# First key block ahead of the queries, and the last shared-expert batch added to the output in one transfer

## The chip, the cores and the metric

The kernel runs on one core of a Trainium2 chip. The core has a matrix engine (TensorE; PE in the profile, and PEld for its weight loads), a vector engine (VectorE, DVE), a scalar engine (ScalarE, ACT), a general engine (GpSimd, POOL) and a sequencer that mostly issues transfers (SyncE, SP). Each works through its own instructions in order. Transfers between HBM (DRAM) and the on-chip memory (SBUF) are DMAs; here they are issued by SP, by ACT and by POOL. Matmuls write into eight PSUM banks.

The metric is the device time of one execution in microseconds (us); lower is better. Three runs of the kernel before gave a median of 1747.25 us (1747.18 to 1747.39).

## What is computed

A transformer layer on x of shape (4, 512, 512): cross-attention over a context of 1601 rows per batch, then a mixture of experts. Both are added to x.

```python
# attention: 16 heads of 32; first 257 context rows are "image", the other 1344 "text"
q     = rms_norm(layernorm(x) @ q_w + q_b) * norm_q_w
k     = rms_norm(text @ k_w + k_b) * norm_k_w ;   v     = text @ v_w + v_b
k_img = rms_norm(img @ k_img_w + ...) * ...   ;   v_img = img @ v_img_w + ...
x = x + (softmax(q k^T / sqrt(32)) v + softmax(q k_img^T / sqrt(32)) v_img) @ o_w + o_b

# experts: T = 2048 tokens, 32 experts of inner size 256, 4 chosen per token, at most 80 slots each
h = layernorm(x)
slots_token, slots_w = route(sigmoid(h @ router_w.T))
Y   = (silu(h[slots_token] @ W_gate) * (h[slots_token] @ W_up)) @ W_down * slots_w
out = zeros(T, 512).at[slots_token].add(Y)
shared = (silu(h @ shared_gate.T) * (h @ shared_up.T)) @ shared_down.T      # inner size 512
x = x + out + shared
```

All matrices are float32.

## The kernel before

The kernel has three stages.

**Opening.** `first_x` loads the four 128-row tiles of batch 0's x on SP, then `q_w` comes in four pieces of 256 KB, then `k_w`, the first context block and `v_w` as whole transfers of 1 MB. ACT issues the small bias and norm columns and `o_b` (nine DMAs). `queries` gives for each x tile three closures: `measure` (mean and variance on DVE, the root on POOL), `norm` (ACT, L265), `turn` (four PE transposes at L271 and one ACT copy at L272). All four tiles are normed and turned one after the other; after that the four query chunks run (`part`, `feature_chunk`, L223: four k-steps each, moving 512 columns, so each needs all four tiles turned). Only then begins the loop over batches with the keys of block 0. A float32 matmul shows up as two instructions in the profile.

`feature_chunk` ends with a square on ACT (L227), a scaled copy on DVE (L228) and a sum of squares on POOL (L230). `norms` (N in the table `side`) turns sums of squares into roots; `normed` (M) multiplies them in; `scores` (W) computes the score maxima. `side` says after which (block, chunk) of the keys each is called. The x tiles, normed tiles and squares share a ring `rowt` of five buffers.

**Attention.** Four batches; PE runs through scores, exponentials and weighted sums almost without a gap. `routing(b, space)` chooses the experts for one batch on DVE; its `space` is scratch. `routing_constants` prepares four small tensors for it.

**Experts.** `shared()` cuts the shared expert into units: for each batch of 512 rows eight gate/up units and four down units, each 16 matmuls. The units of batches 0 to 2 and batch 3's residual run ahead of the experts. The twelve units of batch 3 are kept in `between` and dealt among the routed experts by the condition at L1072. Each of the last four (`down(j)`) copies PSUM to `ys` on ACT (L945) and adds 256 KB to `out` with a POOL DMA that accumulates (L946).

A routed expert e passes through: `gather` (POOL, indirect DMA of 80 rows, issued `AHEAD` experts early), `turn` (PE transposes, L976), `gate_up` (PE, L217; ACT and DVE), `down` (PE L995; ACT copy to `y`, L999; POOL indirect DMA adding 80 rows of 2 KB to `out`, L1000, called the scatter below). `y` has three buffers. Expert weights (1.5 MB each) come over SP into `WEIGHTS` = 5 buffers. All adds to `out`, scatters and `ys` alike, touch the same tensor, so each waits until the one before has landed; that chain is called the chain of adds below. On POOL's queue the gather of a later expert stands behind the scatter that is called before it.

Of the kernel before, what the change touches and what calls it, by code (L numbers as in the profile page):

```python
# [9 lines left out]
F32 = mybir.dt.float32  # L10
# [3 lines left out]
ALU = mybir.AluOpType  # L14
# [4 lines left out]
P = 128  # L19
# [90 lines left out]
def body(ctx, tc, a, ident, mhalf, logits, x1_d, xw_d, xnT_d, den_d, rec_d, out):  # L110
# [39 lines left out]
    def held(name):  # L150
        return hold.tile([P, D], F32, name=name, tag="hold")
# [6 lines left out]
    def bias_column(name):  # L158
        return column(name, a[name].rearrange("(c p) -> p c", p=P))
# [3 lines left out]
        nc.sync.dma_start(t, a[name])  # L163
        return t

    def load_x(b, qt):
        xt = rowt("xt")
        nc.sync.dma_start(xt, a["x"][b, qt * P:(qt + 1) * P, :])
        return xt

    def load_block(b, bl):
# [2 lines left out]
        nc.sync.dma_start(cT, a["ctxT"][b, :, s0:s0 + n].rearrange("(c p) t -> p c t", p=P))  # L174
        return cT

    first_x = [load_x(0, qt) for qt in range(NQ)]
    wq = w.tile([P, NC, D], F32, name="q_w")
    for k in range(NC):
        nc.sync.dma_start(wq[:, k, :], a["q_w"][:, k, :])  # L180
    q_b, nq_w = bias_column("q_b"), column("norm_q_w")
    k_b, nk_w = bias_column("k_b"), column("norm_k_w")
    first_wk = weight("k_w", wide("wk"))
    first_block = load_block(0, 0)
    wv = weight("v_w")
    ki_b, nki_w = bias_column("k_img_b"), column("norm_k_img_w")
    v_b, vi_b = bias_column("v_b"), bias_column("v_img_b")
# [434 lines left out]
    qT, sq_q, turn, work = queries(0, first_x, L)  # L622
    for measure, _, _ in turn:
        measure()
    for _, norm, turned in turn:
        norm()
        turned()
    nc.vector.tensor_scalar(nq_w, nq_w, SM_SCALE, None, ALU.mult)
    for f in work:
        f()  # L630
    ident_b = w.tile([P, P], BF16, name="ident_b")
    nc.vector.tensor_copy(ident_b, ident)

# [24 lines left out]
        parts.append(t)  # L658

    nc.vector.tensor_tensor(v_b, v_b, vi_b, ALU.add)  # L660
    routing_constants()
    select, search = [], []
    pending = []
    for b in range(B):
        kT = kv.tile([P, NC, S], F32, name="kT")
        v = kv.tile([P, NKT, P], F32, name="v", bufs=2)
        wk = first_wk if b == 0 else weight("k_w", wide("wk"))
        cTs = [first_block if b == 0 else load_block(b, 0), load_block(b, 1)]
        wki = weight("k_img_w", wide("wki"))
        rest = [[]] * NQ  # L670
        if b == 0:
# [7 lines left out]
        ws = (wv, wvi)  # L679
        mx = st.tile([P, NQ, NG4, NM], F32, name="mx", tag="mx", bufs=2)  # L680
        sqs, rs = {"q": sq_q}, {}

        if b > 1:
            space = kv.tile([P, NC, L], F32, name="space", tag="xlT")
            select, search = routing(b - 2, space.rearrange("p c t -> p (c t)"))
# [34 lines left out]
        def due():  # L720
# [22 lines left out]
            (3, 2): [W(1, 3)],  # L743
            (3, 3): [W(2, 0)],
        }
        for bl in range(NB):
            for c in range(NC):
                keys(bl, c)
                for f in side.get((bl, c), ()):
                    f()  # L750

                n = 7 if bl < 2 else 0
                for f in select[:n]:
                    f()
                del select[:n]
                later.step()
# [126 lines left out]
        return ws  # L883

    SHARE = 2.4
    AHEAD, WEIGHTS = 6, 5

    def tokens():

# [7 lines left out]
    def shared():  # L897


        units = [[], []]  # L900
        downs = []
        xTs = {0: first_xT[0]}

        def fetch_x(n):
            xTs[n] = wide("xT")
            nc.sync.dma_start(xTs[n], xnT_d[:, :, n * L:(n + 1) * L])

        for n in range(B):
            t = {}

            def gate(ic, n=n, t=t):
                if ic == 0:
                    t["hT"] = wide("hT")
                if ic == 2 and n + 1 < B:
                    fetch_x(n + 1)
                ps = psum()
                project(ps, lambda k: sg[:, k, ic * P:(ic + 1) * P], lambda k: xTs[n][:, k, :])
                nc.scalar.activation(t["hT"][:, ic, :], ps, AF.Silu)

            def up(ic, n=n, t=t):  # L920
                ps = psum()
                project(ps, lambda k: su[:, k, ic * P:(ic + 1) * P], lambda k: xTs[n][:, k, :])
                nc.vector.tensor_tensor(t["hT"][:, ic, :], t["hT"][:, ic, :], ps, ALU.mult)
                if n == 0 and ic == NC - 1:
                    wides.append(first_xT[1])

            def fetch(j, n=n, t=t):
                t[j] = held("x1r")
                nc.sync.dma_start(t[j], x1_d[n * L + j * P:n * L + (j + 1) * P, :])

            def down(j, n=n, t=t, fetch=fetch):
                rows = slice(n * L + j * P, n * L + (j + 1) * P)
                if n < BEFORE:
                    if j == 0:
                        fetch(0)
                    if j + 1 < NQ:
                        fetch(j + 1)
                ps = psum()
                project(ps, lambda k: t["hT"][:, k, j * P:(j + 1) * P], lambda k: sd[:, k, :])
                if n < BEFORE:  # L940
                    nc.vector.tensor_tensor(t[j], t[j], ps, ALU.add)
                    nc.sync.dma_start(out[rows, :], t[j])
                else:
                    y = held("ys")
                    nc.scalar.copy(y, ps)  # L945
                    nc.gpsimd.dma_start(out[rows, :], y, accum_op=ALU.add)  # L946

            to = units[n >= BEFORE]
            if n == BEFORE:
                units[0] += downs  # L950
                downs = []
            for ic in range(NC):
                to += [partial(gate, ic), partial(up, ic)]
                if ic < 2:
                    to += downs[2 * ic:2 * ic + 2]
            downs = [partial(down, j) for j in range(NQ)]
        units[1] += downs
        return units

    def expert_parts():  # L960
        weights, xps, xpTs, hs = {}, {}, {}, {}

        def gather(e):
            xps[e] = ew.tile([CAP, D + E], F32, name="xp", bufs=AHEAD + 2)
            nc.gpsimd.indirect_dma_start(
                out=xps[e][:, :],
                out_offset=None,
                in_=xw_d[:, :],
                in_offset=bass.IndirectOffsetOnAxis(ap=tok[:, e:e + 1], axis=0),
            )  # L970

        def turn(e):
            ps = psum()
            px = ps[:, :NC * CAP].rearrange("p (c t) -> p c t", c=NC)
            for c in range(NC):
                nc.tensor.transpose(px[:, c, :], xps[e][:, c * P:(c + 1) * P], ident[:CAP, :CAP])  # L976
            xpTs[e] = ew.tile([P, NC, CAP], F32, name="xpT")
            nc.vector.tensor_copy(xpTs[e], px)

        def gate_up(e):  # L980
            ps = psum()
            pg = ps[:, :2 * NI * CAP].rearrange("p (j i t) -> p j i t", j=2, i=NI)
            for j in range(2):
                for ic in range(NI):
                    project(
                        pg[:, j, ic, :], lambda k: weights[e][j][:, k, ic * P:(ic + 1) * P], lambda k: xpTs[e][:, k, :]
                    )
            hs[e] = ew.tile([P, NI, CAP], F32, name="ehT")
            nc.scalar.activation(hs[e], pg[:, 0], AF.Silu)  # L989
            nc.vector.tensor_tensor(hs[e], hs[e], pg[:, 1], ALU.mult)  # L990

        def down(e):
            ps = psum()
            for ic in range(NI):
                nc.tensor.matmul(  # L995
                    ps[:CAP, :], lhsT=hs[e][:, ic, :], rhs=weights[e][2][:, ic, :], start=ic == 0, stop=ic == NI - 1
                )
            y = ew.tile([CAP, D], F32, name="y")
            nc.scalar.mul(y, ps[:CAP, :], xps[e][:, D + e:D + e + 1])  # L999
            nc.gpsimd.indirect_dma_start(  # L1000
                out=out[:, :],
                out_offset=bass.IndirectOffsetOnAxis(ap=tok[:, e:e + 1], axis=0),
                in_=y[:, :],
                in_offset=None,
                bounds_check=T - 1,
                oob_is_err=True,
                compute_op=ALU.add,
            )

        return weights, gather, turn, gate_up, down  # L1010
# [3 lines left out]
    for u in units[:2]:  # L1014
# [8 lines left out]
    tok = ew.tile([CAP, E], I32, name="tok", bufs=1)  # L1023
    weights, gather, turn, gate_up, down = expert_parts()
    rest = [residual(B - 1, qt, aoT_last, lambda: wo) for qt in range(NQ)]
    first, second = (
        select + search
        for select, search in (routing(b, rp.tile([P, 1024], F32, name=f"space{b}")) for b in (B - 2, B - 1))
    )
    O_AT = 8  # L1030
    side = {}
    for qt in range(NQ):
# [4 lines left out]
    for i, u in enumerate(units):  # L1037
# [10 lines left out]
        for f in side.get(i, ()):  # L1048
            f()
        later.step()  # L1050

        while spent < (i - 1) * SHARE and (first or i > ready and second):
            todo = first or second
# [7 lines left out]
    for e in range(E + 1):  # L1061
# [6 lines left out]
        if e:  # L1068
            down(e - 1)
            if e + WEIGHTS - 1 < E:  # L1070
                weights[e + WEIGHTS - 1] = expert_weights(e + WEIGHTS - 1)
        while done < n_between and done * (E - 8) < n_between * (e + 1):  # L1072
            between.pop(0)()
            done += 1

# [36 lines left out]
```

## Time and profile before

The profiled execution took 1747.46 us; its span, from the first to the last instruction, is 1745.7 us. All rows below are of that execution, times from the span's start.

| What | Value |
|---|---|
| median of three runs | 1747.25 us |
| profiled execution / span | 1747.46 / 1745.7 us |
| PE busy, DVE, ACT, POOL (share of the span) | 97%, 56%, 37%, 50% |
| first x tile landed (first DVE statistics) | 4.07 us |
| first query matmul | 18.84 us |
| last of batch 0's block 0 and query matmuls | 51.1 us |
| first expert matmul | 1495.74 us |
| last PE instruction ends | 1723.2 us |
| last scatter issued | 1737.92 us |

The page names, for each group of instructions, its line, engine, operation, output and inputs; the timeline lists them in order of time, with the idle time ahead of each in brackets and what ended it. A busy PE counts modelled ends, so that short pauses between matmuls don't show.

### The profile page before, as it was taken

The numbers are of one execution on the slowest core, as the hardware profiler recorded it, in microseconds if no ns is written. First come the engines' busy times: TensorE is split into PE (matmuls) and PEld (weight loads), VectorE is DVE, ScalarE is ACT, GpSimd is POOL, SyncE is SP. The second block draws the span as 40 slices with busy tenths as digits, with TensorE's granted clock in tenths as the row PEclk, the third lists the DMA queues.
The fourth block names the chain that finished last, engine by engine and source line by source line (L and its number), as shares of the span: only waits on it lengthen the run. The fifth ranks groups of instructions, "written<-read, shape, count | busy, mean of one in ns | idle before, by whom it ended". The sixth has DMA issues, their size and how long they took to land. (4 is left out here: it accounts for less than half of the span.)

```text
span 1745.7 us, 29525 instructions
## 1 busy us (share of the span) xinstructions
PE 1694.6 (97%) x11825; PEld 893.7 (51%) x11825; DVE 982.5 (56%) x2016; ACT 650.5 (37%) x1378; POOL 866.9 (50%) x618
## 2 busy tenths in 40 slices
PE   6999999999999999999999999999999999999984
PEld 3564444446544444565444445644443454677763
DVE  2675555758555548976666579676557666111100
ACT  2124556621354566114555641145557110011111
POOL 2328879332569763336688533286792110333232
PEclk9999999999999999999999999999999999999997
DMA  6000000221100004020000040300012462688882
GB/s 228 1 2 1 26 20 8 93 82 55 43 2 26 26 3 150 26 79 19 5 23 26 15 149 20 103 13 14 2 39 86 159 229 86 204 264 265 262 253 38
DMA packets 67912, 137.34 MB, mean 79 GB/s; under 512 B 16064, under 2 KB 28480, under 8 KB 65600
## 3 DMA queue, kind: packets, MB, share of 16 engines
q1 hardware_dynamic: 58720, 123.30, 20.8%
q0 software_dynamic: 5696, 11.87, 3.3%
q8 instruction: 93, 1.52, 0.4%
q10 hardware_dynamic: 3360, 0.30, 0.1%
q14 instruction: 43, 0.35, 0.1%
HBM read 112.63 MB, written 22.81 MB: 78 GB/s over the span
## 5 line engine op out<-in xcount | busy, mean ns | idle before, releaser
L366 ACT ACTIVATE pT<-ps 128x512 f32<-128x512 f32 (+1 forms) x832 | 429.7, 603 | 342.2 <-PE ps L365 334.1
L328 DVE TENSOR_REDUCE mx<-ps 128x1 f32<-128x512 f32 (+1 forms) x576 | 331.3, 617 | 264.8 <-PE ps L314 264.8
L381 POOL TENSOR_TENSOR acc<-acc,pT 128x1024 f32<-128x1024 f32 x192 | 445.7, 2359 | 3.0 <-ACT pT L366 2.6
L373 PE MATMUL po<-pT,v 128*32 128x512 f32 (+2 forms) x1792 | 222.0, 603 | 0.0
L284 PEld LDWEIGHTS ps<-v_w,cT 128*128 128x128 f32 (+1 forms) x1408 | 168.9, 186 | 102.2 <-DVE mx L328 56.1
L365 PE MATMUL ps<-qT,kT 32*128 32x512 f32 (+1 forms) x1664 | 213.7, 587 | 0.0
L314 PE MATMUL ps<-kT,qT 32*128 32x512 f32 (+1 forms) x1536 | 206.2, 549 | 0.0
L284 PE MATMUL ps<-v_w,cT 128*128 128x128 f32 (+1 forms) x1408 | 197.7, 284 | 0.0
L223 PE MATMUL ps<-cT,wk 128*128 128x512 f32 (+1 forms) x384 | 153.7, 545 | 0.0
L302 DVE TENSOR_REDUCE mx<-ps 128x1 f32<-128x512 f32 (+2 forms) x256 | 128.3, 564 | 5.7 <-PE ps L299 5.6
L1000 POOL DMA_INDIRECT out<-y,tok x32 | 45.7, 1428 | 143.9 <-ACT y L999 55.6
L990 DVE TENSOR_TENSOR ehT<-ehT,ps 128x160 f32<-128x160 f32 x32 | 10.3, 322 | 181.9 <-ACT ehT L989 148.2
L362 PEld LDWEIGHTS <-pick 32*128 32x128 bf16 (+1 forms) x832 | 21.6, 91 | 165.8 <-issue 164.0
L223 PEld LDWEIGHTS ps<-cT,wk 128*128 128x128 f32 x384 | 69.6, 190 | 69.0 <-issue 54.3
L292 ACT COPY v<-ps 128x128 f32<-128x128 f32 (+1 forms) x208 | 59.7, 287 | 118.3 <-PE ps L284 117.8
L230 POOL TENSOR_TENSOR sq_k<-sq_k,sq 128x512 f32<-128x512 f32 (+2 forms) x48 | 49.7, 1035 | 105.3 <-ACT sq L227 105.1
L388 POOL TENSOR_TENSOR acc<-pT 128x1024 f32<-128x1024 f32 x24 | 56.2, 2361 | 87.1 <-ACT pT L366 54.5
L381 POOL TENSOR_TENSOR pT<-pT 65x1024 f32<-65x1024 f32 x24 | 56.0, 2355 | 86.5 <-PE po L373 77.8
L381 DVE TENSOR_TENSOR acc<-acc,pT 128x1024 f32<-128x1024 f32 (+1 forms) x72 | 97.8, 1405 | 2.1 <-ACT pT L366 2.1
L314 PEld LDWEIGHTS ps<-kT,qT 32*128 32x128 f32 x1536 | 82.0, 183 | 30.8 <-issue 10.1
L373 PEld LDWEIGHTS po<-pT,v 128*32 128x32 f32 (+2 forms) x1792 | 34.7, 107 | 118.6 <-issue 109.3
L362 PE MATMUL ps<-mT,pick 32*128 32x512 bf16 (+1 forms) x832 | 82.5, 385 | 2.5 <-ACT mT L353 2.5
(176 smaller groups left out, 2220.0 us busy)
## 6 DMA issues: line engine op xcount, KB each, us to landing
W_gate<-in_W_gate SPq DMA_DIRECT2D x32, 512.0 KB
W_up<-in_W_up SPq DMA_DIRECT2D x32, 512.0 KB
W_down<-in_W_down SPq DMA_DIRECT2D x32, 512.0 KB
xt<-in_x SPq DMA_DIRECT2D x32, 256.0 KB
cT<-in_ctxT SPq DMA_DIRECT2D x8, 1024.0 KB
rb<-rec_d SPq DMA_DIRECT2D x64, 128.0 KB
wk<-in_k_w SPq DMA_DIRECT2D x4, 1024.0 KB
wki<-in_k_img_w SPq DMA_DIRECT2D x4, 1024.0 KB
```

The source lines that it names most:

```text
L223: nc.tensor.matmul(ps[:, :n], lhsT=wt[:, k, c * P:(c + 1) * P], rhs=xT[:, k, to], start=k == 0, stop=k == NC - 1)
L284: nc.tensor.matmul(ps[lo:hi, :], lhsT=cTs[bl][:, k, at:at + hi - lo], rhs=ws[bl == NB - 1][:, k, c * P:(c + 1) * P], start=k == 0, stop=k ...
L292: nc.scalar.copy(v[:n, t, :], ps[:n])
L302: nc.vector.tensor_reduce(mx[:, qt, g, bl:bl + 1], ps[:, :n], AX.X, ALU.max, negate=True)
L314: nc.tensor.matmul(ps[:, j * n:(j + 1) * n], lhsT=qT[r:r + HD, c, q * P:(q + 1) * P], rhs=kT[r:r + HD, c, k0:k0 + n], start=True, stop=True,)
L328: nc.vector.tensor_reduce(mx[:, qt, g, i:i + 1], ps[:, :m], AX.X, ALU.max, negate=True)
L362: nc.tensor.matmul(ps[:n], lhsT=pick[r:r + HD, kind(t), :n], rhs=mT[r:r + HD, :], start=True, stop=False)
L365: nc.tensor.matmul(ps[:n], lhsT=kT[r:r + HD, c, t * P:t * P + n], rhs=qT[r:r + HD, c, :], start=False, stop=True)
L366: nc.scalar.activation(pT[:n, g, :], ps[:n], AF.Exp)
L373: nc.tensor.matmul(po[r:r + HD, :], lhsT=v[rows, t, r:r + HD], rhs=pT[rows, g, :], start=start, stop=stop)
L381: (nc.vector if idle else nc.gpsimd).tensor_tensor(to[rows, h, :], to[rows, h, :], pT[rows, h, :], ALU.add)
L388: (nc.vector if idle else nc.gpsimd).tensor_tensor(acc[:, h, :], pTs[0][:, h, :], pTs[1][:, h, :], ALU.add)
```

## The change

Four parts of the kernel are edited.

1. Opening: `k_w` and the first context block come in four pieces each, `k_w` on ACT's queue and the block on SP's, with the four x tiles dealt between them (two on each queue). Four PSUM banks are opened for the keys of block 0, and the matmuls run k-step by k-step over all four chunks; norms and turns of x are called between the k-steps. In the batch loop, block 0's place in batch 0 is taken by the four query chunks, and `side` swaps the N and M of block 0 and of the queries.
2. `routing_constants` is called at the start of batch 1. The scratch of the two last routings changes: one tile is left in the pool, and the second routing uses `rb`'s buffer.
3. Shared expert of batch 3: the four copies go into one tile `ys` of 1 MB, and the fourth is followed by a single accumulating DMA of 1 MB.
4. Expert loop: `AHEAD` 6 to 7, `y` with 4 buffers, and `between` dealt at `E - 15` where it was `E - 8`.

```diff
-    first_x = [load_x(0, qt) for qt in range(NQ)]
+    first_wk = wide("wk")
+    _, n, s0, _ = BLOCKS[0]
+    first_block = cx.tile([P, NC, n], F32, name="cT0", tag="cT0")
     wq = w.tile([P, NC, D], F32, name="q_w")
+    first_x = []
+    for k in range(NC):
+        nc.scalar.dma_start(first_wk[:, k, :], a["k_w"][:, k, :])
+        nc.sync.dma_start(first_block[:, k, :], a["ctxT"][0, k * P:(k + 1) * P, s0:s0 + n])
+        if k in (1, 2):
+            first_x += [load_x(0, len(first_x), nc.scalar), load_x(0, len(first_x) + 1)]
     for k in range(NC):
         nc.sync.dma_start(wq[:, k, :], a["q_w"][:, k, :])
+    k_b, nk_w = bias_column("k_b"), column("norm_k_w")
     q_b, nq_w = bias_column("q_b"), column("norm_q_w")
-    k_b, nk_w = bias_column("k_b"), column("norm_k_w")
-    first_wk = weight("k_w", wide("wk"))
-    first_block = load_block(0, 0)
+    second_block = load_block(0, 1)
...
-    for _, norm, turned in turn:
-        norm()
-        turned()
-    nc.vector.tensor_scalar(nq_w, nq_w, SM_SCALE, None, ALU.mult)
-    for f in work:
-        f()
+    first_kT = kv.tile([P, NC, S], F32, name="kT")
+    first_banks = [psum() for _ in range(NC)]
+    for k in range(NC):
+        if k == NC - 1:
+            first_sq = rowt("sq_k")
+            nc.vector.tensor_scalar(nq_w, nq_w, SM_SCALE, None, ALU.mult)
+        for c, ps in enumerate(first_banks):
+            feature_chunk(first_kT[:, :, :n], first_block, n, first_wk, k_b, nk_w, c, ps, first_sq if k == NC - 1 else None, k)
+        if k == 0:
+            turn[0][1]()
+            turn[1][1]()
+        if k == 2:
+            for qt in (0, 1):
+                turn[qt][2]()
+                turn[qt + 2][1]()
+    for qt in (2, 3):
+        turn[qt][2]()
...
+        if b == 0:
+
+            side.update({(0, 0): [N(0)], (0, 1): [], (0, 2): [M(0)], (1, 0): [N("q")], (1, 2): [M("q")]})
         for bl in range(NB):
             for c in range(NC):
-                keys(bl, c)
+                if b == 0 and bl == 0:
+                    work[c]()
+                else:
+                    keys(bl, c)
...
-    AHEAD, WEIGHTS = 6, 5
+    AHEAD, WEIGHTS = 7, 5
...
-                else:
-                    y = held("ys")
-                    nc.scalar.copy(y, ps)
-                    nc.gpsimd.dma_start(out[rows, :], y, accum_op=ALU.add)
+                    return
+                if j == 0:
+                    t["ys"] = wide("ys")
+                nc.scalar.copy(t["ys"][:, j, :], ps)
+                if j == NQ - 1:
+                    to = out[n * L:(n + 1) * L, :].rearrange("(j p) d -> p j d", p=P)
+                    nc.gpsimd.dma_start(to, t["ys"], accum_op=ALU.add)
...
-            y = ew.tile([CAP, D], F32, name="y")
+            y = ew.tile([CAP, D], F32, name="y", bufs=4)
...
-        while done < n_between and done * (E - 8) < n_between * (e + 1):
+        while done < n_between and done * (E - 15) < n_between * (e + 1):
```

More of the change, by code (lines that the diff above doesn't have):

```diff
@@ L164, in weight, with load_x @@
         return t
-    def load_x(b, qt):
+    def load_x(b, qt, queue=nc.sync):
         xt = rowt("xt")
-        nc.sync.dma_start(xt, a["x"][b, qt * P:(qt + 1) * P, :])
+        queue.dma_start(xt, a["x"][b, qt * P:(qt + 1) * P, :])
         return xt
@@ L660, in body @@
     nc.vector.tensor_tensor(v_b, v_b, vi_b, ALU.add)
-    routing_constants()
     select, search = [], []
@@ L664, in body @@
     for b in range(B):
-        kT = kv.tile([P, NC, S], F32, name="kT")
+        kT = kv.tile([P, NC, S], F32, name="kT") if b else first_kT
         v = kv.tile([P, NKT, P], F32, name="v", bufs=2)
         wk = first_wk if b == 0 else weight("k_w", wide("wk"))
-        cTs = [first_block if b == 0 else load_block(b, 0), load_block(b, 1)]
+        cTs = [load_block(b, 0), load_block(b, 1)] if b else [first_block, second_block]
         wki = weight("k_img_w", wide("wki"))
@@ L681, in body @@
         sqs, rs = {"q": sq_q}, {}
+        if b == 0:
+            sqs[0] = first_sq
+        if b == 1:
+            routing_constants()
         if b > 1:
@@ L745, in body @@
         }
+        if b == 0:
+            side.update({(0, 0): [N(0)], (0, 1): [], (0, 2): [M(0)], (1, 0): [N("q")], (1, 2): [M("q")]})
         for bl in range(NB):
             for c in range(NC):
-                keys(bl, c)
+                if b == 0 and bl == 0:
+                    work[c]()
+                else:
+                    keys(bl, c)
                 for f in side.get((bl, c), ()):
@@ L1025, in body @@
     rest = [residual(B - 1, qt, aoT_last, lambda: wo) for qt in range(NQ)]
[L1026 to L1029, printed above, removed]
+    first, second = sum(routing(B - 2, rp.tile([P, 1024], F32, name="space")), []), None
     O_AT = 8
@@ L1050, in body @@
         later.step()
+        if i == ready:
+            space = mid.tile([P, 2, L], F32, name="rb")
+            second = sum(routing(B - 1, space.rearrange("p k t -> p (k t)")), [])
         while spent < (i - 1) * SHARE and (first or i > ready and second):
```

## The prediction

> **What bounds the kernel now.** I read the page first: PE is busy almost everywhere, except in the first and the last slice of 40, where its clock is below full as well.
>
> ```profile
> PE 1694.6 (97%) x11825; PEld 893.7 (51%) x11825; DVE 982.5 (56%) x2016; ACT 650.5 (37%) x1378; POOL 866.9 (50%) x618
> ...
> PE   6999999999999999999999999999999999999984
> ...
> PEclk9999999999999999999999999999999999999997
> ```
>
> So a change can gain only at the two ends; between them PE's work is the same, and an earlier start moves all of it. Next the timeline of the opening.
>
> ```profile
> 7.38 1.28 ACT L265 ACT_TABLE_LOAD   x1 [7.38 <-DMA norm_k_img_w<-in_norm_k_img_w]
> ...
> 9.54 1.12 PE L271 MATMUL ps<-ident,xl 128*128 128x128 f32 x4 [9.54 <-ACT xl L265]
> ...
> 18.84 16.82 PE L223 MATMUL ps<-xlT,q_w 128*128 128x512 f32 x32 [0.68 <-ACT xlT L272]
> 19.86 0.33 PEld L223 LDWEIGHTS ps<-xlT,q_w 128*128 128x128 f32 x1 [0.52 <-issue]
> ...
> 25.21 0.19 PEld L223 LDWEIGHTS ps<-xlT,q_w 128*128 128x128 f32 x1 [0.24 <-issue]
> ```
>
> PE does sixteen transposes in 18.84 us, each four waiting for ACT. Then a weight load comes every 0.86 us until 24.5 us and every 0.43 us after it: PE starts at half clock, which costs 5.7/2 = 2.8 us. Last, POOL's timeline of the end, with PE's last row.
>
> ```profile
> 1618.84 1.42 POOL L1000 DMA_INDIRECT out<-y,tok  x1 [4.88 <-DMA out<-y,tok]
> 1624.64 0.96 POOL L946 DMA_DIRECT2D out<-ys  x1 [4.38 <-issue]
> ...
> 1632.95 1.48 POOL L1000 DMA_INDIRECT out<-y,tok  x1 [6.04 <-DMA out<-ys]
> ...
> 1688.01 0.96 POOL L946 DMA_DIRECT2D out<-ys  x1 [3.34 <-DMA out<-y,tok]
> ...
> 1695.44 1.47 POOL L1000 DMA_INDIRECT out<-y,tok  x1 [5.18 <-DMA out<-ys]
> 1700.16 1.43 POOL L1000 DMA_INDIRECT out<-y,tok  x1 [1.99 <-ACT y L999]
> ...
> 1733.22 1.40 POOL L1000 DMA_INDIRECT out<-y,tok  x1 [3.26 <-DMA out<-y,tok]
> 1737.92 1.40 POOL L1000 DMA_INDIRECT out<-y,tok  x1 [3.30 <-issue]
> ```
>
> ```profile
> 1719.64 3.60 PE L995 MATMUL ps<-W_down,ehT 128*80 128x512 f32 x8
> ```
>
> PE is done at 1723.2 us; the chain of adds ends 22.5 us later. From the scatter at 1611.30 on it has no pause: each add is issued when the one before has landed. So the end is set by the adds still to come, not by PE.
>
> The intervals tell the price of an add. With no weights in flight a scatter takes 4.67 us. SP's timeline shows 1.5 MB of weights issued per expert; where they fill the interval it is 7.5, 7.5, 8.3 and 7.5 us, where they fill some half of it 5.8 to 5.9. A `ys` add takes 8.31, 7.47, 7.78 and 7.43.
>
> **Opening.** Cost step by step, on PE:
> - 512 KB (a piece of `k_w` and one of the block) must land. The first x tile, 256 KB issued at 0.80, was in by 4.07; I put two at 4.8 us, after which PE starts, 14.0 us earlier than the first query matmul.
> - k-step 0 is 8 instructions at 0.86 = 6.9 us less the part after warming: to 11.1. Steps 1 and 2 at 8 x 0.43 = 3.4 each: to 17.9.
> - The transposes of tiles 0 and 1 now stand in PE's line and wait for `norm` on ACT. ACT issues six pieces before its nine columns. In the trace its sixth issue comes at 4.07, when the first x lands, and SP's fourth x at 4.32: three of SP's and five of ACT's were then open, so eight at once seem to be the limit. So ACT's issues go at the pace of landings. 3 MB at 271 GB/s (windows view, 0 to 20 us) is 11.6 us; the columns come after it, and I put the end of ACT's issues at 16 us (7.35 before). The table load follows (1.28), then the norms at 0.81 and copies at 0.59: tile 0 is normed at 18.1, so PE waits a few tenths; two tiles are turned by 19.5, k-step 3 runs to 22.9.
> - ACT, whose first copy ends at 19.6, still owes two norms and a copy (2.2), four squares (0.69 each, 2.8) and two copies (1.2): 25.8. Query chunk 0 needs the last copy: it starts at 25.9, after a PE pause of 2 us.
> - Four query chunks (13.7) and an N and M (1.65) end at 41.3. Before, the same work ended at 51.1.
>
> **Gain 9.8 us.** If ACT is no hindrance the 2 us go too (12); if ACT is done only at 21 us, it is 5 us less (5). Late pieces matter little: k-step 3 does not begin before 19.5.
>
> Here a rule speaks against dealing over two queues. The row: SP issued three x tiles, then stood from 2.1 to 4.3 us, and ACT's tiny columns held open slots. The Trainium skill, "DMA: Bandwidth & Descriptors", section "Issuing engines are not separate DMA queues", says that transfers from several issuers share the same 16 engines, so that only issue time is saved. By the rule the pieces still take 11.6 us for 3 MB, the last at some 14 us; by the row (the columns no longer first) they may come sooner. Either way step 3 begins at 19.5: the sum is 9.8 by both, and the rule leaves only ACT's lost time as the price, which is in it.
>
> What is late next: N and M of block 0 meet DVE's 6.8 us of small memsets (37.15 to 43.9 in the trace), now at about 25 to 32; M(0) is called at 36, so these stay hidden. The swapped N("q"), M("q") stand as far from W(0,0) as M(0) did; its wait of 1.0 us stays.
>
> **Small edits.** The constants (ACT 0.35, POOL 0.63, DVE 0.12 us) move behind PE's unbroken work of batch 1; the routing scratch changes no operation, the wait of 0.31 us ahead of L600 stays. A seventh gather ahead is 1.2 us on POOL at 1498, after the gather that PE needs first. Each of these: nothing.
>
> **The end.** An expert round on PE is 3.53 + 0.28 + 1.72 = 5.53 us, a shared unit 3.43. With `E - 15` the twelve units fall in rounds 0 to 15: 16 x 5.53 - 1.7 + 12 x 3.43 = 128 us after 1495.7, so the fourth copy is at 1624. The scatter of expert 14 is in flight, so the 1 MB add goes at about 1627, with 17 scatters after it. Before, at 1624.64, there were four `ys` adds and 16 scatters to come.
> - Price Y of the 1 MB add; no row shows it. The trace's DMA packets of a `ys` add are 128 of 2 KB, spread over 2.3 to 3.1 us of its 7.4 to 8.3: about 5 us are fixed. Four times 2.7 is 10.8; with some 1 us for a longer descriptor list, **Y = 16.5**. Lower end: the same page, section "Anatomy of one DMA", fits 2.0 us + bytes/436 GB/s = 4.4. The row refutes it: for 256 KB it gives 2.6 where the trace has 7.4. Upper end: four full adds, 4 x 7.43 to 4 x 8.31 = 30 to 33.
> - Queued behind: POOL's scatter of expert 15 and the gathers. A gather is now issued five rounds (27 us) before its turn, and four `y` buffers cover four rounds, so PE hardly stands during the add.
> - Afterwards the chain paces PE. Without units in between, PE asks for weights every round; scatters 15 to 22 meet transfers of 5 us in an interval of 7, so between 5.9 and 7.7: 7.1 each, 57 us. Weights are then through, since PE is four `y` ahead. Scatters 23 to 30: 8 x 4.67 = 37.4. From the last scatter to the end 7.8 as before.
> - Sum: 1627 + 16.5 + 57 + 37.4 + 7.8 = 1745.7, **change 0**.
>
> In short: three fixed shares of 5 us go, and are given back by one more scatter after the add, its later issue, and costlier scatters, because the shared units no longer space them. By a cheap Y (4.4) it would be -12; by 33 it would be +16.
>
> **Sum.** The profiled execution is 1747.46 = span 1745.7 + 1.8 outside; less 9.8 gives 1737.7, and the median lies 0.2 under it: **1737 us** in round numbers.
>
> **Rivals.**
> - Cheap add: Y near 4 to 9; end 8 to 12 us sooner, 1725 to 1730. For: POOL's own issue is only 0.96. Against: the 7.4 us rows. 0.14.
> - ACT late: 21 us or more until it is free; gain 5, 1742; for it the trace's ACT issues at 1.2 us each from 4.07 on, against it the columns' own small size. 0.14.
> - Slow add, the other sign: place, the wait of scatter 15 on the 1 MB add; price 33; +16 at the end against -9.8: 1754. It decides above 26: then faster turns slower. For: adds read and write HBM and ran at that rate four times. Against: 5 of 7.4 us look fixed. 0.11.
> - Forecast, 1731 to 1743: 0.61.
>
> The edit of the end shows in one DMA for four, so that it does nothing is no case.
>
> Faster and slower count from 0.2% (3.5 us), about what a measurement of this kernel can tell from no change. Faster: forecast, cheap add and a bit over half of ACT late, 0.82; same 0.08 with the upper tail of the forecast; slower 0.10. The range 1727 to 1746 leaves out the best half of cheap add and the slow add.
>
> **What would show it.** Right: first L223 near 4.8 us, first query chunk near 26, block 0 and queries done near 41; one L946 near 1617 (all shifted by 10) and the next scatter 16 to 17 us later; then intervals of about 7, last nine 4.67. Wrong: a wait of PE on L265 of several us; a wait behind L946 under 10 or over 26 us; scatters at 7.5 to the end; PE idle on gathers for more than a few us while the chain is not behind.

## The result and the profile after

The changed kernel takes 1739.42 us (median of six runs, 1737.32 to 1741.86), against 1747.32 of the kernel before (1742.58 to 1749.19). The ratio is 0.9958, 95% interval 0.9944 to 0.9972: faster by about 7.3 us (4.9 to 9.8). The profiled execution took 1738.34; its span is 1736.6 us, 9.1 less than before.

The page of the changed kernel, its rows of PE and clock in 40 slices, looks much as before: PE's first slice is fuller by two tenths, the one before the last by one, and the last is emptier by one.

```profile
PE 1688.6 (97%) x11825; PEld 890.4 (51%) x11825; DVE 982.7 (57%) x2016; ACT 649.4 (37%) x1378; POOL 865.2 (50%) x615
...
PE   8999999999999999999999999999999999999993
...
PEclk9999999999999999999999999999999999999997
```

The timeline of the opening, PE and ACT (start, length, what; in brackets the idle time ahead and what ended it):

```profile
6.06 12.06 PE L231 MATMUL ps<-cT,wk 128*128 128x512 f32 x24 [6.06 <-DMA wk<-in_k_w]
18.53 0.66 PE L279 MATMUL ps<-ident,xl 128*128 128x128 f32 x4 [0.41 <-ACT xl L273]
19.43 0.66 PE L279 MATMUL ps<-ident,xl 128*128 128x128 f32 x4 [0.24 <-ACT xl L273]
19.92 3.60 PE L231 MATMUL ps<-cT,wk 128*128 128x512 f32 x8
23.36 1.04 PE L279 MATMUL ps<-ident,xl 128*128 128x128 f32 x8
26.00 3.70 PE L231 MATMUL ps<-xlT,q_w 128*128 128x512 f32 x8 [1.60 <-ACT xlT L280]
...
41.62 3.60 PE L231 MATMUL ps<-cT,wk 128*128 128x512 f32 x8
```

```profile
16.37 1.28 ACT L273 ACT_TABLE_LOAD   x1 [16.37 <-DMA k_img_b<-in_k_img_b]
```

PE now starts on the keys at 6.06 us, waits twice for a normed tile and once for the last copy, and has block 0 and the queries done at 41.6 us; before, that was at 51.1. So 9.5 us are gained within the first 42 us. At the first expert matmul 9.4 of them are still there (before, it started at 1495.74), so nothing in between gained or lost:

```profile
1486.30 2.01 PE L225 MATMUL ps<-xpT,W_gate 128*128 128x80 f32 x16 [0.62 <-issue]
```

The span is shorter by 9.1, so the end has neither gained nor lost. PE's last row and POOL's timeline there:

```profile
1706.45 1.94 PE L1026 MATMUL ps<-W_down,ehT 128*80 128x512 f32 x4 [1.48 <-DVE ehT L1021]
```

```profile
1612.16 1.42 POOL L1031 DMA_INDIRECT out<-y,tok  x1 [4.46 <-ACT y L1030]
1618.83 1.41 POOL L977 DMA_DIRECT2D out<-ys  x1 [5.25 <-ACT ehT L1020]
1620.55 1.02 POOL L996 DMA_INDIRECT xp<-xw_d,tok  x1 [0.30 <-issue]
1633.71 1.48 POOL L1031 DMA_INDIRECT out<-y,tok  x1 [12.13 <-DMA out<-ys]
...
1642.36 1.43 POOL L1031 DMA_INDIRECT out<-y,tok  x1 [5.93 <-issue]
...
1691.88 1.42 POOL L1031 DMA_INDIRECT out<-y,tok  x1 [3.06 <-ACT y L1030]
1696.61 1.41 POOL L1031 DMA_INDIRECT out<-y,tok  x1 [3.31 <-issue]
...
1729.06 1.39 POOL L1031 DMA_INDIRECT out<-y,tok  x1 [3.32 <-DMA out<-y,tok]
```

One add where there were four, with 14.88 us from its issue to the next scatter's. Behind it stand 17 scatters: the first eight intervals (1633.71 to 1691.88) are 7.3 us each, the next eight 4.65. PE is done at 1708.4, and the kernel ends 28 us after it; before it was 22.5. So PE is done 15 us earlier than before, but the chain of adds, which ends the kernel, only 9.

### The profile page after: what moved, and what is told of

Same layout as the page of the kernel before. It is cut to its first block, busy times and chain, and to the rows that moved or that the text cites. A ratio compares the mean times of both kernels' runs of the same rounds, so it can differ in the third digit from the quotient of the medians.

```text
span 1736.6 us, 29529 instructions
## 1 busy us (share of the span) xinstructions
PE 1688.6 (97%) x11825; PEld 890.4 (51%) x11825; DVE 982.7 (57%) x2016; ACT 649.4 (37%) x1378; POOL 865.2 (50%) x615
## 5 line engine op out<-in xcount | busy, mean ns | idle before, releaser
L1021 DVE TENSOR_TENSOR ehT<-ehT,ps 128x160 f32<-128x160 f32 x32 | 10.3, 322 | 177.2 <-ACT ehT L1020 162.8
```

## Experiments

All ratios are to the kernel before, run beside each kernel on the same chip.

**Each end alone.** The first kernel has the new opening and the old end:

```diff
-    AHEAD, WEIGHTS = 7, 5
+    AHEAD, WEIGHTS = 6, 5
...
-                if j == 0:
-                    t["ys"] = wide("ys")
-                nc.scalar.copy(t["ys"][:, j, :], ps)
-                if j == NQ - 1:
...
+                y = held("ys")
+                nc.scalar.copy(y, ps)
+                nc.gpsimd.dma_start(out[rows, :], y, accum_op=ALU.add)
...
-            y = ew.tile([CAP, D], F32, name="y", bufs=4)
+            y = ew.tile([CAP, D], F32, name="y")
...
-        while done < n_between and done * (E - 15) < n_between * (e + 1):
+        while done < n_between and done * (E - 8) < n_between * (e + 1):
```

> The new opening (with the moved constants and the smaller routing scratch) and the old end: four 256 KB adds, AHEAD 6, three y buffers, E - 8. Theory: the whole change of time is in the opening, so this gains 9 to 10 us, some 1738 against 1747, and the last scatter is issued about as long after the first expert matmul as before (242 us). Rival, that the end pays and the opening's gain is lost to later waits: within 3 us of before.

The second has the old opening and the edits of the expert loop, the add and the routing scratch:

> The old opening and the new end: one 1 MB add, AHEAD 7, four y buffers, E - 15, with the smaller routing scratch that makes room for them. Theory: what the one add saves, the earlier and closer scatters give back: change between -2 and +2 us, some 1747. Rival, that the end pays: 5 us or more faster.

Measured: the opening alone 1739.16 us, ratio 0.9943 (0.9926 to 0.9959); the end alone 1748.58, ratio 0.9999 (0.9991 to 1.0008). The changed kernel has 0.9958. The whole change of time is in the opening; the end is a draw to within a tenth of a per cent, and within their intervals the two add up. The smaller routing scratch comes along with the end, to leave room for the fourth `y` buffer and the ninth gather buffer; it was not tried apart.

**What an add costs.** The chain's intervals could be long because an accumulating DMA is slow by itself, or because weights move beside it. This kernel uses the weights of the first five experts again and again, so that later ones are not loaded (its result is then not the layer's):

```diff
     def expert_weights(e):
+        if e >= WEIGHTS:
+            return weights[e % WEIGHTS]
         ws = []
```

> The changed kernel with the weights of the first five experts only: later experts use them again and load none (27 x 1.5 MB left out). Theory: the length of the adds comes from the weight traffic beside them: all scatters after the 1 MB add follow at 4.6 to 4.8 us or at PE's 5.5 us, the 1 MB add takes 11 to 13 us, and the kernel ends some 10 us after PE, near 1720 to 1724. Rival, that an add is slow by itself: the scatters after the 1 MB add still take 6 to 8 us.

Measured: 1719.19 us (one execution), just below the 1720 to 1724 expected. POOL's timeline of it:

```profile
1618.53 1.41 POOL L979 DMA_DIRECT2D out<-ys  x1 [3.07 <-issue]
...
1628.31 1.48 POOL L1033 DMA_INDIRECT out<-y,tok  x1 [7.04 <-ACT y L1032]
1630.09 0.94 POOL L998 DMA_INDIRECT xp<-xw_d,tok  x1 [0.30 <-issue]
1632.98 1.43 POOL L1033 DMA_INDIRECT out<-y,tok  x1 [1.94 <-issue]
...
1637.69 1.41 POOL L1033 DMA_INDIRECT out<-y,tok  x1 [2.04 <-ACT ehT L1022]
```

The 1 MB add falls from 14.88 to 9.78 us (11 to 13 had been expected). (The profile puts the first scatter's wait down to ACT, but that is the `y` of the next expert; its own was ready at 1622.7.) The scatters behind it are 4.8 us apart in the mean of seven, where they were 7.3. By then the chain has caught up with PE, and the later ones follow PE at 5.5 us. The windows view gives the traffic (us; busy time of PE, PEld, DVE, ACT and POOL; clock, share of the DMA engines, GB/s), first of the changed kernel from the add to scatter 23, then of this one:

```profile
1620.00:1634.00 14.00, 14.00 (x109) 11.84 (x108) 1.45 (x4) 2.66 (x5) 1.56 (x3) 1.00 1.00 254
1634.00:1690.00 56.00, 53.86 (x386) 42.82 (x385) 6.49 (x18) 7.64 (x17) 18.61 (x16) 1.00 0.97 324
```

```profile
1629.00:1690.00 61.00, 61.00 (x445) 49.13 (x443) 7.93 (x22) 10.87 (x22) 24.49 (x21) 1.00 0.34 56
```

With the weights beside them, and the DMA engines full (0.97 to 1.00), the adds take some 50% longer than without. After the last shared unit PE, at 5.5 us per expert, asks for weights so fast that they slow the adds on which the end depends.

Two adds of 512 KB ask how the price goes with size:

```diff
-                if j == NQ - 1:
-                    to = out[n * L:(n + 1) * L, :].rearrange("(j p) d -> p j d", p=P)
-                    nc.gpsimd.dma_start(to, t["ys"], accum_op=ALU.add)
+                if j % 2:
+                    to = out[n * L + (j - 1) * P:n * L + (j + 1) * P, :].rearrange("(j p) d -> p j d", p=P)
+                    nc.gpsimd.dma_start(to, t["ys"][:, j - 1:j + 1, :], accum_op=ALU.add)
```

> The changed kernel with two adds of 512 KB, after the second and the fourth shared down unit. Theory: an add costs a fixed part of about 5 us and the rest by its bytes, so that each takes 10 to 11 us in the profile (7.4 to 8.3 at 256 KB, 14.9 at 1 MB); the first falls where the chain still has slack, so 2 to 5 us slower than the changed kernel. Rival, that the length goes by bytes alone: each 7 to 8 us, and no slower than the changed kernel.

Measured: 1738.83, ratio 0.9949 (0.9932 to 0.9965); the adds take 10.90 and 9.20 us (1597.65 to 1608.55, 1628.53 to 1637.73). The price is about as expected: 7.4 to 8.3 us for 256 KB, some 10 for 512 KB, 14.9 for 1 MB, so roughly 5 us and 10 us per MB. The time is not: it is no slower than the changed kernel. Scatter 15 does go 4.0 us later (1637.73), but the eight intervals behind it sum to 53.6 us where they were 58.2. A part of that can be chance: two of the kernels below that leave the end as in the changed kernel have 54.1 (ACT free) and 57.1 (one queue). Why they are shorter here is not shown.

Four adds of 256 KB, with the rest of the changed kernel kept (the diff of the opening alone, its `ys` part only):

> The changed kernel with four 256 KB adds again, dealt at E - 15. Theory: four adds of 7.4 to 8.3 us in place of one of 14.9, partly while the chain has slack between the shared units: 6 to 10 us slower than the changed kernel, some 1746 to 1749. Rival, that the chain recovers by the end whatever the adds cost: within 2 us of the changed kernel.

Measured: 1746.93, ratio 0.9981 (0.9966 to 0.9997): 7.5 us over the changed kernel in the median, but only 4 by the ratios, whose intervals overlap. Its twelve executions spread from 1737.00 to 1750.29 us; the twelve of the end alone lie within 6.2, the six of the changed kernel within 4.5. The profile is of one that took 1739.4; there the adds took 6.6 to 7.8 us, less than the 7.4 to 8.3 of the kernel before. So with the units dealt at `E - 15` four adds can come out as well as one and mostly do not. What decides it from one execution to the next stays open.

**Where the shared units go.** One number back:

```diff
-        while done < n_between and done * (E - 15) < n_between * (e + 1):
+        while done < n_between and done * (E - 8) < n_between * (e + 1):
```

> The changed kernel with one number back: E - 8, so the twelve shared units are dealt over 24 rounds and the 1 MB add comes after expert 22. Theory: scatters spaced by shared units meet less weight traffic, and fewer are left after the add: 6 to 9 us faster than the changed kernel, some 1731 to 1733. Rival, that the early add is needed so that the chain can recover: slower than the changed kernel by 5 us or more.

And the other way, `E - 4`:

> The changed kernel with the shared units dealt at E - 4, over 28 rounds; the 1 MB add then comes after expert 26, when hardly any weights are left to load. Theory: the scatters before it are spaced by shared units to the end, and only five come after it, at 4.67 us each: 1 to 4 us faster than with E - 8 (1730.85), some 1728. Rival, that an add of some 12 to 15 us so near the end can't be recovered: 3 us or more slower than with E - 8.

Measured: 1730.85 with `E - 8`, ratio 0.9899 (0.9882 to 0.9915), and 1729.49 with `E - 4`, ratio 0.9893 (0.9877 to 0.9910). POOL's timeline with `E - 4`:

```profile
1671.20 1.41 POOL L1031 DMA_INDIRECT out<-y,tok  x1 [6.20 <-DMA out<-y,tok]
1676.70 1.39 POOL L977 DMA_DIRECT2D out<-ys  x1 [4.08 <-DMA out<-y,tok]
1692.62 1.50 POOL L1031 DMA_INDIRECT out<-y,tok  x1 [14.53 <-ACT ehT L1020]
1697.30 1.42 POOL L1031 DMA_INDIRECT out<-y,tok  x1 [3.19 <-DMA out<-y,tok]
...
1720.66 1.39 POOL L1031 DMA_INDIRECT out<-y,tok  x1 [3.29 <-DMA out<-y,tok]
```

The add takes 15.92 us here, more than in the changed kernel, and behind it come seven scatters (I had expected five) at 4.67, for the weights are nearly through: their last issue is at 1682.6. But the gain is not made there. It lies before expert 15, where the changed kernel's chain waits for PE:

```profile
1565.26 1.42 POOL L1031 DMA_INDIRECT out<-y,tok  x1 [6.06 <-ACT y L1030]
1574.22 1.42 POOL L1031 DMA_INDIRECT out<-y,tok  x1 [6.31 <-ACT y L1030]
1582.12 1.42 POOL L1031 DMA_INDIRECT out<-y,tok  x1 [5.25 <-DMA out<-y,tok]
```

```profile
1573.26 0.68 ACT L1030 ACTIVATE y<-ps,xp 80x512 f32<-80x512 f32 x1 [1.74 <-PE ps L1026]
```

An expert round with a shared unit takes PE 5.53 + 3.43 = 8.96 us, longer than a scatter takes to land. With `E - 15` ten units fall into the first fourteen intervals. Eleven of the first fifteen scatters are issued within 0.6 us of the end of their `y`; from expert 15 on every `y` lies ready for 13 to 22 us, and where the profile still names ACT, the copy is that of a later expert into the buffer just freed. With `E - 8` seven units fall there, with `E - 4` six:

| Chain of adds | `E - 15` | `E - 8` | `E - 4` |
|---|---|---|---|
| scatter 0 to scatter 14 | 111.8 | 101.5 | 98.0 |
| scatter 14 to scatter 31, with the add | 116.9 | 119.1 | 120.6 |

The first row differs by 10.3 and 13.7 us, three and four units of 3.43. The second row gives a little back. So dealing the units early, at `E - 15`, is what cost the gain of the single add: they delay the first `y`s, and the chain can't make up for the wait later. The scatters themselves are no cheaper with `E - 8`: the 21 intervals before its add are 7.28 us each, the eight behind the add of the changed kernel 7.27. At `E - 8` the single add does pay: the opening alone, with four adds at `E - 8` (and the smaller buffers), has a ratio of 0.9943, the changed kernel with `E - 8` 0.9899, and the intervals are apart.

`E - 4` is 1.4 us below `E - 8`; this difference lies within their intervals.

**Buffers.** AHEAD 6 and three `y` buffers, all else as changed:

> The changed kernel with AHEAD 6 and three y buffers. Theory: the chain of adds sets the end, not PE, so that PE stands longer but the time is within 2 us of the changed kernel. Rival, that the extra buffers are what keeps the 1 MB add from stopping PE and so the kernel: 3 us or more slower.

Measured: 1740.02, ratio 0.9951 (0.9935 to 0.9968), no difference to be seen. PE ends later (1715 us), and the last scatter goes at 1731.0 where it went at 1729.1.

**The opening.** All pieces on SP's queue:

```diff
-        nc.scalar.dma_start(first_wk[:, k, :], a["k_w"][:, k, :])
+        nc.sync.dma_start(first_wk[:, k, :], a["k_w"][:, k, :])
...
-            first_x += [load_x(0, len(first_x), nc.scalar), load_x(0, len(first_x) + 1)]
+            first_x += [load_x(0, len(first_x)), load_x(0, len(first_x) + 1)]
```

> The changed kernel with all twelve pieces (key weights, block and x) issued by SP; ACT issues the columns only. Theory: the same 16 engines move the pieces and eight open DMAs are the limit either way, so the first key matmul starts at 6 us plus or minus 0.7 and the time is within 2 us of the changed kernel. Rival, that two queues bring the pieces sooner: first key matmul later by 1 us or more and k-steps that wait, 2 us or more slower.

Measured: 1741.29, ratio 0.9958 (0.9943 to 0.9972), as the changed kernel. Its timeline:

```profile
5.88 13.15 PE L231 MATMUL ps<-cT,wk 128*128 128x512 f32 x24 [5.88 <-DMA cT<-in_ctxT]
...
26.23 3.70 PE L231 MATMUL ps<-xlT,q_w 128*128 128x512 f32 x8 [2.02 <-ACT xlT L280]
```

```profile
9.09 1.28 ACT L273 ACT_TABLE_LOAD   x1 [9.09 <-DMA xt<-in_x]
```

Two things are in it. The pieces do come more slowly: the windows view has 251, 176 and 181 GB/s from 6 to 12 us, where the changed kernel has 404, 397 and 374, probably because ACT's columns now go out first, ahead of most pieces; the order and the number of queues changed together, so this is not shown. PE does not feel it. And ACT is free at 9.1 us, 7 earlier than in the changed kernel, yet PE's pause ahead of the queries is still there, 2.0 us against 1.6. In ACT's own order the norms of tiles 2 and 3 stand behind a copy that waits for PE's transposes, and these stand behind k-step 2; so it is this order and not ACT's DMA issues that makes the pause.

So both are put right together: columns and `o_b` on SP, all norms after k-step 0, all turns after k-step 2.

```diff
-        nc.scalar.dma_start(t, a[name] if src is None else src)
+        nc.sync.dma_start(t, a[name] if src is None else src)
...
         if k == 0:
-            turn[0][1]()
-            turn[1][1]()
+            for qt in range(NQ):
+                turn[qt][1]()
         if k == 2:
-            for qt in (0, 1):
+            for qt in range(NQ):
                 turn[qt][2]()
-                turn[qt + 2][1]()
-    for qt in (2, 3):
-        turn[qt][2]()
```

> The changed kernel with ACT's columns and o_b issued by SP, all four norms called after k-step 0 and all four turns after k-step 2. Theory: ACT is free at some 9 us, where it was free at 16.4, PE waits no longer for norms and copies, and the first query chunk starts at 23 to 24 us, where it was 26.0: 2 to 3 us faster than the changed kernel, some 1737. Rival, that the pieces set the pace and not ACT: within 1 us of the changed kernel, with PE waiting for pieces.

Measured: 1737.32, ratio 0.9941 (0.9924 to 0.9958), 2.1 us under the changed kernel in the median, though the intervals of the ratios overlap. The order alone, with ACT's issues as in the changed kernel, was not tried. PE has no pause left:

```profile
5.94 13.64 PE L231 MATMUL ps<-cT,wk 128*128 128x512 f32 x24 [5.94 <-DMA wk<-in_k_w]
19.42 1.91 PE L279 MATMUL ps<-ident,xl 128*128 128x128 f32 x16
21.17 3.60 PE L231 MATMUL ps<-cT,wk 128*128 128x512 f32 x8
24.61 3.60 PE L231 MATMUL ps<-xlT,q_w 128*128 128x512 f32 x8
```

The query chunk starts at 24.61, somewhat later than expected, because PE's half clock lasted longer in this execution (below); in the next kernel, with the same opening, it starts at 23.70.

**Both gains.** This opening with `E - 4`:

> The changed kernel with both gains: ACT free of the columns, all turns after k-step 2, and the shared units dealt at E - 4. Theory: the two are at different ends and add up, 9.9 us (E - 4) and 2.1 us (ACT free) under the changed kernel: 1727 to 1728. Rival, that the earlier start is eaten by the chain at the end: 1729.5, as with E - 4 alone.

Measured: 1726.84, ratio 0.9878 (0.9861 to 0.9894). In the medians they add up, as expected (2.6 us under `E - 4` alone, with overlapping intervals). It is the fastest kernel here, 21 us under the kernel before and 12.6 under the changed one.

## Why the prediction was right

The forecast was 1737.7 us for a profiled execution and 1737 for the median; the profiled one took 1738.34, the median is 1739.42. The profiled execution is the second fastest of the six, so the rows below flatter the forecast by about a microsecond.

**Opening, forecast -9.8, measured -9.5 at 42 us.** One reading was wrong: the clock's row shows a digit below 9 only in the last slice, not in the first, in both kernels. It is the weight loads, 0.86 us apart and then 0.43, that show the half clock at the start. Almost every step stood where it was put.

| Step | forecast | measured |
|---|---|---|
| first key matmul | 4.8 | 6.06 |
| end of k-step 2 | 17.9 | 18.1 |
| ACT's issues end | 16 | 16.3 |
| k-step 3 ends | 22.9 | 23.4 |
| first query chunk | 25.9 | 26.00 |
| block 0 and queries done | 41.3 | 41.6 |

Two terms were off and cancel, which is luck. The first pieces came 1.3 us later than I had put them; and PE's half clock, which I had taken as 5.7 us from before, lasted 3.2 us in this execution, which gives 1.2 us back. The reason given for PE's pause was only half right: I had tied it to ACT's issues ("If ACT is no hindrance the 2 us go too"). With ACT free early and the order kept, the pause stays; with the order changed as well it goes, and 2.1 us with it.

On the rule against two queues: the rate of the pieces did rise to 1.6 to 2.3 times the one-queue kernel's between 6 and 12 us. Whether open slots were short is not shown: the windows view has the DMA engines 0.77 to 0.97 busy there with one queue too, so that the columns' small packets may as well have held them. The time did not move, as the sum had it, because k-step 3 waits for nothing that the pieces bring.

**End, forecast 0, measured +0.4** (9.5 us earlier at 42 us, 9.1 at the end), and 0.9999 where it was tried alone.

| Term | forecast | measured |
|---|---|---|
| issue of the 1 MB add (9.8 us earlier start taken off) | 1617.2 | 1618.83 |
| Y | 16.5 | 14.88 |
| scatters 15 to 22 | 57 | 58.2 |
| scatters 23 to 30 | 37.4 | 37.2 |
| last scatter to the end | 7.8 | 7.5 |

A later issue and a shorter add cancel here, and that is luck of this execution. Four other kernels with the same single add at `E - 15` have Y = 14.7 (buffers), 16.50 (one queue), 16.65 (end alone) and 16.66 (ACT free), so the forecast of 16.5 is within what one add varies. In the profiled execution its 512 packets lie over 11.5 us, four times the 2.3 to 3.1 of a `ys` add before, so 3.4 us were fixed; the forecast had 10.8, and 5.7 fixed. The packets begin 2.0 us after the issue here, and 4.5 to 4.8 us after it in the last three of the others; why is not shown. The estimate from the fit that the Trainium skill gives ("DMA: Bandwidth & Descriptors", section "Anatomy of one DMA"), 4.4 us, is far off even with the weights gone (9.78), and so is four times the small add (30 to 33).

Against the kernel before, the sum comes out as named: one add for four gives 16.1 us; it goes 3.6 us later, counted from the first expert matmul; and sixteen intervals of scatters behind it take 95.4 us, where before fifteen took 82.3. But the reason given for the dear scatters, that the shared units no longer space them, is not borne out: with `E - 8` they are spaced and 7.28 us apart all the same, and without weights 4.8. And what the forecast counted as a later issue and one more scatter has a cause that it did not name: from scatter 0 to scatter 14 the changed kernel's chain takes 10.3 us more than before (111.8 against 101.5), because it waits for `y`s that PE makes later.

```profile
1509.83 1.51 POOL L1000 DMA_INDIRECT out<-y,tok  x1 [12.06 <-ACT y L999]
...
1611.30 1.42 POOL L1000 DMA_INDIRECT out<-y,tok  x1 [2.58 <-ACT y L999]
```

These are the scatters 0 and 14 of the kernel before; in the changed kernel they go at 1500.38 and 1612.16.

**Small edits at nothing.** AHEAD and the `y` buffers measured as no difference; the constants and the scratch were not tried apart, but 9.4 of the 9.5 us gained at 42 us are still there at the first expert matmul, so neither cost anything to be seen.

**Rivals.** The cheap add is out by its wait of 14.88. ACT late did not happen: it was free at 16.4. The slow add is out as well; above 26 us it would have turned the sign, and the longest seen, with `E - 8`, is 17.6 (1658.98 to 1676.57).

## What to carry to other kernels

When transfers that must follow each other end a kernel, look at when each becomes ready and at what else moves beside it: here each took half as long again beside the weights (7.3 us against 4.8). Work that feeds few of them (the shared units, twelve for one add) should not stand ahead of work that feeds many: dealt early, it held the chain up while the chain had nothing else to do; dealt over 24 or 28 rounds, the kernel was 8.6 and 9.9 us faster. Before an engine is blamed for a wait, ask what stands ahead of the awaited instruction in its own order: freeing ACT did nothing until its work was reordered too.

## Not expected of the hardware

- **The half clock at the start lasts differently in each execution**: from PE's first projection matmul to the change of spacing from 0.86 to 0.43 us it is 5.7 us in the profile before (where transposes had run since 9.54), 3.2 in the changed kernel and 6.3 in the one with ACT free, worth up to 1.6 us. The Trainium skill, "TensorE: Matmul & The Clock Gate", section "Part 1: The HAM clock gate", says that the activity window runs free of the kernel, so that the moment of the change varies; the 0.5 us either way that it gives for this is less than the spread here.
- **Eight open DMAs, whichever queue issued them**, seem to be the limit in this program's opening: in the changed kernel SP and ACT issue four each by 2.7 us, and the ninth goes at 5.86, about when the first piece is in. By this count a bias column of 2 KB holds one of the eight as a 256 KB piece does: with one queue SP has issued three pieces and ACT five columns by 3.4 us, and the ninth goes at 4.48.
- **An accumulating DMA of 256 KB took 7.4 to 8.3 us** in the kernel before, though its packets lie over 2.3 to 3.1 us of that.
